# Second thread's state sums by transposes, and its first block prepared inside the leading thread's first layer

## The chip, the cores and the metric

The kernel runs on one core of a Trainium2 chip. The metric is the device time of one execution in microseconds (us). Before the change it was 4766.82 us, the median of three runs (4752.45, 4766.82 and 4772.51).

The engines go by short names. PE is TensorE with its matmuls, PEld its weight loads, DVE is VectorE, ACT is ScalarE, POOL is GpSimd, and SP is SyncE, whose queue issues almost all DMAs here.

## The reference, cut to what matters

A residual stream `x` of 8 sequences, 256 tokens and 256 features passes through twelve layers, each `x = x + layer(layernorm(x))`, with a context of 77 tokens beside it in some. All of it is in float32. The change concerns the first layer, a state-space layer that runs forwards and backwards:

```
def _s6(u, A_log, D, Wx, Wdt, bdt):
    A = -jnp.exp(A_log)
    dbc = jnp.einsum('bld,ed->ble', u, Wx)            # 64 of dt, 16 of B, 16 of C
    ...
    delta = jax.nn.softplus(jnp.einsum('blr,dr->bld', dt, Wdt) + bdt)
    dA = jnp.exp(delta[..., None] * A)
    dBu = delta[..., None] * Bm[:, :, None, :] * u[..., None]
    ...
        h = dA_t * h + dBu_t
        y = jnp.einsum('bdn,bn->bd', h, C_t)
    ...
    return ys + u * D
```

`u` is the input projection to 512 channels, convolved causally over four tokens and passed through Silu. Each of the 512 channels has 16 states. The two directions are added, multiplied by a gate (the Silu of the other half of the input projection) and by one half, and projected back to 256 features. The second layer is a cross attention over context and tokens (`perceiver16` in the kernel), the third a mixture of experts (`moe`).

## The kernel before

The eight sequences form four blocks of two (512 tokens each). Two Python generators, called threads here, issue the program: the leading one ("left") takes blocks 0 and 1 through all twelve layers, the second one ("right") blocks 2 and 3. `build` holds a planned time for each thread and always advances the one that is behind. Each `yield` of a layer moves its thread on by a step `dt`, derived from the layer's share in `SHARE`. The second thread starts with a lag of 1.01 x 470 planned units, which is about the planned end of the leading thread's first layer. The order in which instructions are traced is their priority. The tile framework then picks, for each engine, the ready instruction with the highest priority and so fixes each engine's queue; on the chip each queue runs in order. A tile pool hands its buffers out in that order too. Pools lie on the left or the right side of the on-chip memories, one side for each thread, and a new pool reuses the addresses of a closed one on its side, tile by tile.

**The leading thread's first layer** (class `Wide`) has the machine to itself and uses both sides: `net` (left) and `other` (right). `steps` prepares block 0 with `channels` (norm, transposes, projection, convolution by four products with diagonal `taps`, Silu), `rows` (the product with Wx into `dbc`, a copy of its B and C rows to DRAM as `rows0f`, and C turned into `cols`) and `delta` (softplus). After that each block has a forward and a backward "way" of 16 states by two halves. `way` issues half a state, and after it one more step of the `parts` that belong to a later stretch: gated products of the block before, gates of this one, and the channels, rows and delta of the next. In the last way (block 1, backwards) only the gates stand beside the states.

`state` makes, for each of four chunks of 128 channels: `st = exp(dl * A)` in PSUM on ACT (L825), `db = du * B` on POOL (L827), a scan on DVE (L829), and y. For three states out of four y is summed with tokens in rows: PE transposes the state (L854, `ht`), ACT scales it by C (L856, `ys`), and PE transposes it back into the accumulating bank (L859). For each fourth state DVE multiplies by C (L832, `hc`, two buffers), and PE adds the product up with the identity as weights (L833). The other products of this layer share the two `ht` banks through an alias.

**The second thread's first layer** (`ssm`, L541) starts when that one ends. It loads the layer's weights once more (L547), and for each block norms and turns x, projects and convolves (four DVE instructions per chunk, L565 and L569), applies Silu, makes `dbc` and writes the rows to DRAM. In its first block it also zeroes a table of slots for `moe` (`cleared`). Then it takes two chunks at a time (`c0`) and for each direction makes `dl` and `du` (L593 to L608) and 16 states x 2 chunks: a row load `rep` that is broadcast to all partitions (L614), `st` (L618), `db` on POOL (L622), the scan (L623), `hc` (L627, four buffers), and on PE

```
                            nc.tensor.matmul(
                                y[c],
                                lhsT=net.ident,
                                rhs=hc,
                                start=d == "f" and n == 0,
                                stop=d == "b" and n == 15,
                            )
```

at L628: the identity is the weight, hc streams through with 512 columns, and the bank `y[c]` holds channels in rows. The two `mm` banks serve both `st` and every other product of this layer. After both directions the gate is computed (L642), u is combined with y (L643, L646), and after the second pair the block is projected and added to x (`project`, L462).

Meanwhile the leading thread is in `perceiver16` (attention in head pairs; scores `sc`, maximum L966, exponentials L970, scaling L977, transposes L983, `av`), with one PSUM buffer of each kind.

Of the kernel before, what the change touches and what calls it, by code (L numbers as in the profile page):

```python
# [8 lines left out]
F32 = mybir.dt.float32  # L9
U8 = mybir.dt.uint8  # L10
I32 = mybir.dt.int32
AF = mybir.ActivationFunctionType
# [6 lines left out]
C = 77  # L19
# [271 lines left out]
def pairs_of(t):  # L291

    return t.rearrange("p (b t) -> p b t", b=2)


class Base:
# [25 lines left out]

    def load_rest(self):
        for blk in range(1, NB):
            self.load(blk)


class Net:
# [24 lines left out]
    def weights(self, i, split=1):  # L353
# [4 lines left out]
        t = self.work.tile([128, n + m], src.dtype, name=f"w{i}")  # L358
# [153 lines left out]
def context(base, room, net):  # L512
# [3 lines left out]
    rows = room.work.tile([C, B, D], F32, name="rows")  # L516
# [24 lines left out]
def ssm(net):  # L541


    nc = net.nc
    with net.scope(mm=2, y=1):
        work = net.work
        w = net.weights(0, 3)  # L547
# [7 lines left out]
        for blk in net.blks:  # L555
            xt = net.normed_turned(blk, bufs=1)
            u = work.tile([128, 4, 2, S], F32, name="u")
            for c in range(4):
                ps = net.bank()
                net.mms(ps, [(w["W_in"][:, k, c * 128 : c * 128 + 128], xt[:, k, :]) for k in range(2)])  # L560
                u0 = work.tile([128, 2, 3 + S], F32, name="u0", bufs=2)
                nc.gpsimd.memset(u0[:, :, 0:3], 0.0)
                nc.scalar.copy(u0[:, :, 3:], pairs_of(ps))
                acc = work.tile([128, 2, S], F32, name="acc", bufs=2)
                nc.vector.tensor_scalar(  # L565
                    acc, u0[:, :, 0:S], w["conv"][:, c, 0:1], w["b_conv"][:, c : c + 1], ALU.mult, ALU.add
                )
                for k in range(1, 4):
                    nc.vector.scalar_tensor_tensor(  # L569
                        acc, u0[:, :, k : k + S], w["conv"][:, c, k : k + 1], acc, ALU.mult, ALU.add  # L570
                    )
                nc.scalar.activation(u[:, c], acc, AF.Silu)
                yield
            dbc, rows = {}, {}
            for d in "fb":
                ps = net.bank()
                net.mms(pairs_of(ps[:96]), [(w[d + "Wx"][:, c, :], u[:, c]) for c in range(4)])
                dbc[d] = work.tile([96, 512], F32, name="dbc_" + d)
                nc.scalar.copy(dbc[d], ps[:96])

                rows[d] = net.base.dram.tile([32, 512], F32, name=f"rows{blk}{d}")
                nc.sync.dma_start(rows[d], dbc[d][64:96])
            if blk == net.blks[0]:
                yield from cleared(net, net)
            yield
            for c0 in range(0, 4, 2):
                y = [net.ps["y"].tile([128, 512], F32, name=f"y{c}") for c in range(2)]
                for d in "fb":
# [23 lines left out]
                    for n in range(16):  # L612
                        rep = work.tile([128, 2, 512], F32, name="rep", bufs=3)
                        nc.sync.dma_start(rep, by_state[n : n + 1].to_broadcast([128, 2, 512]))  # L614
                        for c in range(2):
# [12 lines left out]
                            nc.tensor.matmul(  # L628
                                y[c],
                                lhsT=net.ident,  # L630
                                rhs=hc,
                                start=d == "f" and n == 0,
                                stop=d == "b" and n == 15,
                            )
                            yield
                for m in range(2):
# [5 lines left out]
                    nc.scalar.activation(res, pairs_of(ps), AF.Silu)  # L642
                    nc.vector.scalar_tensor_tensor(  # L643
                        u[:, c], u[:, c], skip[:, c : c + 1], pairs_of(y[m]), ALU.mult, ALU.add
# [3 lines left out]
            for b in range(2):  # L648
                net.project(blk, b, u[:, :, b], w["W_out"])
                yield  # L650


class Wide:
# [8 lines left out]
    def steps(self):  # L662
        net, nc, other = self.net, self.nc, self.other
# [1682 lines left out]
```

## Time and profile before

| what | value |
|---|---|
| runs shown | 4752.45, 4766.82, 4772.51 us |
| profiled execution, its own time | 4753.15 us |
| its span, first to last instruction | 4751.4 us |
| PE, DVE, ACT, POOL busy | 86%, 56%, 42%, 33% of the span |
| mean granted PE clock | 0.909 |
| last wide scan, first scan of the second thread | 517.1 us, 589.1 us |
| second thread's eight runs of scans | 589.1 to 1306.0 us |
| loads of w0, w0 once more | 1.67 us, 533.5 us |

A line of the groups reads: source line, engine and operation, tiles out and in, shapes, count, then busy time, mean nanoseconds of one, and the idle time just before it with what ended it. A line of a stage table reads: from and to, length, busy time (and count) of each engine, granted clock, share of the DMA engines busy, GB/s. In the timeline a line has its start, its length, the instruction with its count, and in brackets the idle time before it and what ended that. A matmul in float32 appears as two instructions (passes), a transpose as one. Matmuls overlap in PE's pipeline, so a row of several is shorter than their sum.

### The profile page before, as it was taken

How to read it: one execution, taken by the hardware profiler on the slowest of the kernel's cores; microseconds unless marked ns; L12 is line 12 of the kernel's file. 1: busy time of each engine (PE TensorE's matmuls, PEld its weight loads, DVE VectorE, ACT ScalarE, POOL GpSimd, SP SyncE). 2: the span in 40 equal slices, each digit the busy share in tenths (PEclk: the TensorE clock that was granted, in tenths of full speed). 3: DMA queues.
4: the chain of work that ended last, by engine and by line, in shares of the span. 5: the costliest groups of instructions: out<-in, count | busy, mean ns of one | idle time of the engine just before them, and what ended most of it. 6: DMA issues, size and time to landing. Idle time of an engine off the chain costs nothing.

```text
span 4751.4 us, 54874 instructions
## 1 busy us (share of the span) xinstructions
PE 4087.7 (86%) x20192; PEld 2663.6 (56%) x20192; DVE 2665.2 (56%) x5064; ACT 2004.2 (42%) x4513; POOL 1576.2 (33%) x1373
## 2 busy tenths in 40 slices
PE   7777788887889899988989998788989999877988
PEld 3555433433347566655766665555556767645655
DVE  6768787767841444556254556665473562243355
ACT  6767465656533343432333342422343342233331
POOL 5758454344512411124442333432011001122123
PEclk8989899988989899998989998777889999988999
DMA  3111343233416100001610000100010000001000
GB/s 125 55 33 48 117 112 101 58 90 96 99 57 235 60 1 1 13 3 71 242 42 1 1 32 16 41 14 1 1 47 1 14 36 1 34 25 40 2 18 36
DMA packets 96319, 239.72 MB, mean 50 GB/s; under 512 B 8395, under 2 KB 36403, under 8 KB 85683
## 3 DMA queue, kind: packets, MB, share of 16 engines
q1 hardware_dynamic: 86355, 179.49, 12.2%
q0 software_dynamic: 9696, 56.72, 3.4%
q8 instruction: 160, 2.62, 0.2%
q14 instruction: 108, 0.88, 0.1%
HBM read 216.05 MB, written 20.14 MB: 50 GB/s over the span
## 4 chain that ended last, share of the span: by engine, by line
PE 46%; DVE 11%; POOL 5%; issue 4%; ACT 3%; DMA 1%; POOLq 0%; DVEq 0%; ACTq 0%
PE mm L395 22%; PE sc L395 5%; PE sc L403 5%; PE av L403 3%; PE pt L395 3%; PE o L395 3%; PE mm L983 1%; DVE xn L418 1%; PE mm L403 1%; PE mm L2175 1%; PE mm L428 1%; PE mm L1840 1%; DVE hn_sq L1897 1%; DVE pex L979 1%; POOL m_part L1596 1%
## 5 line engine op out<-in xcount | busy, mean ns | idle before, releaser
L622 POOL TENSOR_TENSOR db<-du,rep 128x512 f32<-128x512 f32 x256 | 320.2, 1271 | 182.6 <-DMA rep<-rows3f 44.2
L827 POOL TENSOR_TENSOR db<-du,rep 128x512 f32<-128x512 f32 x256 | 320.9, 1284 | 105.1 <-DVE h L829 81.9
L387 ACT COPY pv<-mm 111x384 f32<-111x384 f32 (+2 forms) x387 | 197.7, 512 | 331.6 <-PE mm L983 144.6
L395 PE MATMUL mm<-xt,w 128*128 128x512 f32 (+1 forms) x704 | 310.2, 569 | 30.7 <-issue 6.2
L623 DVE TENSOR_TENSOR_SCAN mm<-mm,db 128x512 f32<-128x512 f32 x256 | 310.7, 1222 | 36.7 <-ACT mm L618 20.9
L1333 POOL TENSOR_TENSOR qs<-q,w 128x256 f32<-128x256 f32 x256 | 155.4, 628 | 479.6 <-PE sc L395 479.0
L403 PE MATMUL sc<-k,q 64*128 64x333 f32 (+1 forms) x1152 | 249.5, 492 | 74.0 <-ACT pex L970 36.1
L628 PE MATMUL y<-hc,consts 128*128 128x512 f32 x512 | 279.1, 651 | 38.0 <-DVE hc L627 37.9
L403 PE MATMUL av<-pv,v 111*64 111x256 f32 (+5 forms) x2752 | 255.6, 384 | 16.3 <-ACT pv L387 9.2
L395 PE MATMUL sc<-k,qs 128*128 128x256 f32 x1024 | 265.8, 388 | 3.4 <-ACT ex L1347 1.6
L983 PEld LDWEIGHTS mm<-consts,pex 128*111 128x111 f32 x960 | 146.2, 195 | 195.5 <-issue 52.6
L983 PE MATMUL mm<-consts,pex 128*111 128x128 f32 x960 | 197.0, 316 | 61.8 <-ACT pex L977 18.5
L829 DVE TENSOR_TENSOR_SCAN h<-st,db 128x512 f32<-128x512 f32 x192 | 223.2, 1208 | 41.4 <-ACT st L825 34.4
L395 PE MATMUL mm<-h,sw 128*128 128x256 f32 x1024 | 243.3, 384 | 0.0
L970 ACT ACTIVATE pex<-sc,pnm 128x333 f32<-128x333 f32 x320 | 170.3, 537 | 139.3 <-DVE pnm L966 122.9
L403 PEld LDWEIGHTS sc<-k,q 64*128 64x128 f32 (+1 forms) x1152 | 111.8, 200 | 195.4 <-ACT pex L970 67.9
L395 PE MATMUL mm<-kv,w 128*128 128x256 f32 (+1 forms) x640 | 207.3, 445 | 13.3 <-ACT q L1024 10.8
L416 POOL TENSOR_TENSOR rs<-ve,neghalf 128x4 f32<-128x4 f32 (+1 forms) x57 | 59.2, 1039 | 476.3 <-DVE ve L414 395.1
L395 PEld LDWEIGHTS mm<-h,sw 128*128 128x128 f32 x1024 | 192.7, 193 | 32.9 <-issue 6.9
L395 PEld LDWEIGHTS mm<-xt,w 128*128 128x128 f32 x704 | 133.6, 206 | 136.4 <-issue 82.1
L395 PE MATMUL mm<-w,ao 128*128 128x256 f32 x768 | 197.5, 398 | 12.4 <-DVE x L462 10.8
L395 PEld LDWEIGHTS sc<-k,qs 128*128 128x128 f32 x1024 | 181.7, 192 | 45.2 <-issue 15.9
(482 smaller groups left out, 9073.4 us busy)
## 6 DMA issues: line engine op xcount, KB each, us to landing
rep<-rows2f SPq DMA_DIRECT2D x32, 512.0 KB
rep<-rows2b SPq DMA_DIRECT2D x32, 512.0 KB
rep<-rows3f SPq DMA_DIRECT2D x32, 512.0 KB
rep<-rows3b SPq DMA_DIRECT2D x32, 512.0 KB
w<-in_w SPq DMA_DIRECT2D x12, 1024.0 KB
w<-in_w SPq DMA_DIRECT2D x8, 1025.0 KB
w<-in_w SPq DMA_DIRECT2D x6, 1001.0 KB
w<-in_w SPq DMA_DIRECT2D x6, 838.0 KB
```

The costliest lines, as they stand in the source:

```text
L387: self.nc.scalar.copy(out, in_)
L395: self.nc.tensor.matmul(out, lhsT=lhs, rhs=rhs, start=n == 0, stop=n == len(pairs) - 1)
L403: self.nc.tensor.matmul(out, lhsT=lhs, rhs=rhs, start=start, stop=stop, tile_position=at)
L416: nc.gpsimd.tensor_tensor(rs[:rows], ve[:rows], self.neghalf[:rows, :n], ALU.pow)
L622: nc.gpsimd.tensor_tensor(db, du[:, c, :], rep[:, 0], ALU.mult)
L623: nc.vector.tensor_tensor_scan(st[:, order], st[:, order], db[:, order], 0.0, ALU.mult, ALU.add)
L628: nc.tensor.matmul(y[c], lhsT=net.ident, rhs=hc, start=d == "f" and n == 0, stop=d == "b" and n == 15,)
L827: nc.gpsimd.tensor_tensor(db, du[:, c, :], self.rep[:, 0], ALU.mult)
L829: nc.vector.tensor_tensor_scan(h[:, order], st[:, order], db[:, order], 0.0, ALU.mult, ALU.add)
L970: nc.scalar.activation(ex[:, e, :], sc[:, e, :NK], AF.Exp, bias=nm[:, e : e + 1], accum_out=sm[:, e : e + 1])
L983: nc.tensor.transpose(pt[:CH, j * 128 : j * 128 + 128], ex[:, e, j * CH : (j + 1) * CH], net.ident)
L1333: nc.gpsimd.tensor_tensor(qs[:, kc].rearrange("p n (h t) -> p n h t", h=H), q[:, kc, t0 : t0 + 16].rearrange("p (n t) -> p n t", n=2).unsq ...
```

## The change

It has two parts with what they need.

The second thread's `hc` is no longer streamed through the identity. Each of its four slices of 128 tokens is the weight of a transpose that adds into PSUM, so that the two y banks hold tokens in rows and both chunks of the pair in columns. At the end of the pair ACT copies both banks to SBUF (`yt`), and PE transposes them back before u is combined.

The second thread's block 2 goes through `channels` and `rows` in the leading thread's last way, as its `then` block, and not in `ssm`. Its `cols` and `delta` are left to the second thread, which needs no `cols`. The tiles that are handed over (weights, xt, u, dbc) lie in a new pool `shared` on the right side, which stays open until the second thread's `ssm` ends, so the weights are loaded once. `cleared` moves behind the first direction of the second thread's first pair. The context's `rows` tile takes the buffer of `res`.

```diff
+    def hand(self):
+        self.handed = ExitStack()
+        self.shared = self.handed.enter_context(
+            self.tc.tile_pool(name="shared", bufs=1, side="right", reuse_waits="tile")
+        )
...
 def context(base, room, net):
-    rows = room.work.tile([C, B, D], F32, name="rows")
+    rows = net.work.tile([128, 4, 512], F32, name="res").rearrange("p a (n c) -> p (a n) c", c=D)[:C]
...
 def ssm(net):
-        w = net.weights(0, 3)
+        shared, first = net.base.shared, net.base.first
+        w = first["w"]
...
         for blk in net.blks:
-            xt = net.normed_turned(blk, bufs=1)
...
+            if blk == net.blks[0]:
+                xt, u, dbc, rows = (first[k] for k in ("xt", "u", "dbc", "rows"))
+            else:
+                xt = shared.tile([128, 2, 512], F32, name="xt")
...
-            if blk == net.blks[0]:
-                yield from cleared(net, net)
             yield
             for c0 in range(0, 4, 2):
...
-                            nc.tensor.matmul(
-                                y[c],
-                                lhsT=net.ident,
-                                rhs=hc,
-                                start=d == "f" and n == 0,
-                                stop=d == "b" and n == 15,
-                            )
+                            for i in range(4):
+                                o = i % 2 * 256 + c * 128
+                                nc.tensor.matmul(
+                                    y[i // 2][:, o : o + 128],
+                                    lhsT=hc[:, i * 128 : i * 128 + 128],
+                                    rhs=net.ident,
+                                    is_transpose=True,
+                                    start=d == "f" and n == 0 and c == 0 and i % 2 == 0,
+                                    stop=d == "b" and n == 15 and c == 1 and i % 2 == 1,
+                                    skip_group_check=True,
+                                )
                             yield
+                    if blk == net.blks[0] and not c0 and d == "f":
+                        yield from cleared(net, net)
+                yt = work.tile([128, 4, 2, 128], F32, name="yt")
+                for i in range(2):
+                    nc.scalar.copy(yt[:, 2 * i : 2 * i + 2], y[i].rearrange("p (i c m) -> p i c m", i=2, c=2))
                 for m in range(2):
...
+                    ps = net.bank()
+                    for i in range(4):
+                        nc.tensor.transpose(ps[:, i * 128 : i * 128 + 128], yt[:, i, m, :], net.ident)
                     nc.vector.scalar_tensor_tensor(
-                        u[:, c], u[:, c], skip[:, c : c + 1], pairs_of(y[m]), ALU.mult, ALU.add
+                        u[:, c], u[:, c], skip[:, c : c + 1], pairs_of(ps), ALU.mult, ALU.add
                     )
...
+    net.base.handed.close()
...
 class Wide, steps:
+        self.base.hand()
-            self.w = w = net.weights(0, 3)
+            self.w = w = net.weights(0, 3, self.base.shared)
...
                         parts.append(self.gates(now))
+                        parts += [self.channels(then), self.rows(then, "f"), self.rows(then, "b")]
                         if blk != net.blks[-1]:
-                            parts += [self.channels(then), self.rows(then, "f"), self.rows(then, "b")]
                             parts.append(self.delta(then, "f"))
...
+            self.base.first = dict(now, w=w)
...
+    def of(self, o):
+        return self.net.work if o["blk"] in self.net.blks else self.base.shared
...
 Wide.rows:
         yield
+        if o["blk"] not in net.blks:
+            return
```

Where `Wide` allocates xt, u and dbc it now asks `of(o)` for the pool and takes one buffer there in place of two.

## The prediction

> **What bounds the kernel now.** I read the page first, then a table of stages, then what VectorE (DVE) waits for in the stage that the change touches.
>
> ```profile
> PE 4087.7 (86%) x20192; PEld 2663.6 (56%) x20192; DVE 2665.2 (56%) x5064; ACT 2004.2 (42%) x4513; POOL 1576.2 (33%) x1373
> ...
> L623 DVE TENSOR_TENSOR_SCAN mm<-mm,db 128x512 f32<-128x512 f32 x256 | 310.7, 1222 | 36.7 <-ACT mm L618 20.9
> ...
> L628 PE MATMUL y<-hc,consts 128*128 128x512 f32 x512 | 279.1, 651 | 38.0 <-DVE hc L627 37.9
> ```
>
> By the page PE is the engine to relieve: it is busy 86% of the span, and L628, which the change replaces, is one of its largest groups. The table of stages (us; busy time of PE, PEld, DVE, ACT, POOL; granted clock; DMA share) says something else.
>
> ```profile
> 158.00:292.00 134.00, 108.88 (x497) 65.95 (x496) 88.86 (x88) 98.89 (x143) 79.61 (x67) 0.94 0.14 41
> ...
> 421.00:517.00 96.00, 75.66 (x430) 52.90 (x428) 82.23 (x79) 75.49 (x118) 74.94 (x63) 0.95 0.17 50
> ...
> 531.00:589.00 58.00, 37.58 (x86) 15.64 (x86) 34.81 (x107) 20.22 (x31) 9.21 (x12) 0.75 0.59 204
> ...
> 671.00:735.00 64.00, 53.74 (x178) 23.82 (x176) 61.14 (x76) 39.15 (x83) 39.01 (x32) 0.96 0.46 123
> ...
> 905.00:977.00 72.00, 64.40 (x239) 35.17 (x238) 26.51 (x47) 47.87 (x86) 3.87 (x5) 0.91 0.08 24
> ```
>
> 158:292 and 421:517 are the backward directions of the wide thread's two blocks. 531:589 is the second thread's start. 671:735 is one of its eight runs of 32 scans (two chunks, one direction): DVE is busy 61.1 of 64 us. 905:977 lies between its two blocks. The waits of DVE from 590 to 1310 us (total, times, longest):
>
> ```profile
> DVE mm L623 <- ACT mm L618: 20.9, 39, 1.5
> ...
> DVE hc L627 <- PE y L628: 0.5, 2, 0.3
> ```
>
> In the second thread's ssm DVE sets the pace inside the runs, and it waited for the y sums 0.5 us in 720. Between runs a chain over ACT, DVE and POOL does: the gaps from last to first scan are 15.1 to 16.6 us between directions, 21.2 and 31.7 between chunk pairs, 72.4 between blocks. Only after 1415 us is PE the limit (2970 busy of 3336 us).
>
> **1. The y sums by transposes (L628).** Starts in the timeline give the real cost of a row:
>
> ```profile
> 204.29 0.60 PE L859 MATMUL y<-consts,ys 128*128 128x128 f32 x4
> ...
> 1045.30 1.88 PE L628 MATMUL y<-hc,consts 128*128 128x512 f32 x4
> ```
>
> Four passes of 512 columns take 1.88 us, one alone 0.59, so one takes (1.88-0.59)/3 = 0.43, and an hc, which needs two, 0.86. Four 128-column transposes take 0.60, one alone 0.27, so (0.60-0.27)/3 = 0.11 each and 0.44 for the four that replace an hc. PE gets back 0.42 x 256 = 107 us. Weight loads go from two of 189 ns to four of 141 ns (row L859), beside other PE work: PEld is busy 24 of 64 us in a run. On the second thread's chain this is worth 0: 32 x (1.222 + 0.686) = 61.1 us of DVE work per run stay. Who can use the 107 us is the leading thread, in perceiver16 beside the runs. Bound of its gain: a y pass is on PE 0.86/1.91 = 45% of the time, so its PE work waits 0.45 x 0.43 = 0.19 us on average, afterwards 0.23 x 0.22 = 0.05; with nine dependent PE steps in a head pair and 28 pairs from 590 to 1310 that is up to -35. But its pace does not depend on y: two maxima (L966) in nearly each 20 us of a run, and ten in the 105 us from 1310 to 1415, when there is no y any more. I take -8 for the leading thread.
>
> The clock may answer. PE busy in a run falls from 53.7 to about 53.7 - 32 x 0.42 = 40 of 64 us (63%). Row 531:589, with 65%, has a granted clock of 0.75; row 421:517, where turning transposes (L854, L859) are most of PE's work, has 0.95. I take a small loss, +3 for the leading thread; the full one is a rival. [...]
>
> **2. The end of a chunk pair.** Added, four times: two PSUM copies of 0.59 us on ACT (as L387 copies of 128x512) and eight transposes in two lots of 0.60, ahead of L643; the two mm banks now serve four products in place of two before the next delta gets one. The next pair's first y waits for the copies in place of L643. I take +2 each, +8 on the second thread's chain; bounds 0 (the gates' table load and Silu, L642, are late anyway) and +5 each, +20.
>
> **3. The prologue of block 2 goes.** The last wide scan ends at 517.1, the second thread's first starts at 589.1: 72 us. What remains is the constants and one delta chain, which needs only the wide thread's last st banks and far tiles; a direction gap (15.1 to 16.6 us, the same chain) is the nearest row, so 16 plus 2 for neg_a: 18. The gain is 54, less 3 because DVE then also holds the leading thread's norms (34.8 of 58 us busy): -51. W0 (three loads of 838 KB) is not loaded again: its 2.5 MB stood behind the leading thread's w1 on SP's queue and nobody waited for it at 551.8, when the first product waited for DVE, so 0. The zeroing of the slot table (2.9 MB) moves from 535 us into the gap after the first run, ahead of that direction's first rep loads on the same queue: at 373 GB/s it takes 8 us, the gap is 15.9; +2, bounds 0 and +8.
>
> **4. The same work in the wide thread's last direction.** This is what I look at hardest. The parts added there are channels and two rows; the first block's backward direction has these and a delta besides. From scans to scans it took 133.9 us (158.1 to 292.0), the last direction without them 96.4 (420.6 to 517.1). Ceiling: +37.5. Two DVE stalls are most of it:
>
> ```profile
> 218.81 0.69 DVE L832 TENSOR_TENSOR hc<-st,rep 128x512 f32<-128x512 f32 x1 [10.66 <-PE y L833]
> ...
> 260.15 0.69 DVE L832 TENSOR_TENSOR hc<-st,rep 128x512 f32<-128x512 f32 x1 [12.51 <-PE y L833]
> ```
>
> An hc tile (two buffers) stays occupied because its y product is queued on PE behind the products of channels and rows, which wait for ht banks and ACT. Queued behind it stand the scans, and POOL's db behind those. SP gets two writes of 64 KB between its rep loads, POOL one power of 1.0 us and four memsets of 0.1; they are in the rows' difference. Both stalls come from parts that the change adds: 10.7 + 12.5 = 23; I take +24, bounds 0 (DVE is idle 14% of that direction) and +37.5. Everything behind the direction moves with it: the last gated product and the leading thread's w1 load, which today is issued at 530.7. The context's rows, now in the buffer of res, cost 0: ctx_nrm leaves at 120.2, and res is first written at 183.0.
>
> **The sum.** Second thread: -51 + 24 + 8 + 2 = -17. Leading thread: +24 for its later start; from 551.8 to 577 its products no longer share PE with 32 of the other's passes (32 x 0.43 = 14) and DVE with 17 us of norm and convolution, partly the same time, -17; -8 and +3 from part 1: +2. Behind them PE is 89% busy and serves both, so being ahead in one thread is worth about half: (-17 + 2)/2 = -8. The profiled run took 4753.15 (span 4751.4 and 1.75 around it) and would take 4745. It is near the lowest of the three shown (4752.45); against their median, 4766.82, I forecast **4759**. No change is what a measurement cannot tell from it, 0.5% or 24 us.
>
> **Rivals.** *Freed time is used*: the wide thread takes the preparation almost for nothing (+5), since its last direction has six spare k-steps after the rows, and the leading thread gets all of -35. Second thread -51 + 5 + 8 + 2 = -36; leading thread +5 - 17 - 35 = -47; mean -42: 4725, and 4705 if the PE-bound stretch 905:977 (64.4 of 72) shrinks too. For it: 107 us of the busiest engine. Against: DVE's 0.5 us and the constant pace of L966.
>
> *The clock falls* (the slower side): one mechanism, in the second thread's runs. If PE at 63% gets 0.75, as in 531:589, the leading thread's PE work there (53.74 - 31.8 of y = 22 us a run, some 7 a head pair) grows by 7 x (1/0.75 - 1/0.94) = 1.9 us, over 28 pairs +53 in place of +3, and 905:977 by about 14. Second thread -3, leading +52, mean +25: 4792; at 0.70, 4802. It decides from 0.75 down.
>
> *It does not do what it says*: the prepared delta still waits for tiles of the wide thread or its parts run after the last scan, so the 72 us stay a 72 us prologue in another order: 4767 to 4780.
>
> **Chances.** Forecast 0.49, time used 0.29, clock 0.16, not as said 0.06. Faster by over 0.5%: 0.29 + 0.01 of the forecast = 0.30. Slower: 0.16 + 0.02 of the last = 0.18. The rest, 0.52, within. The range leaves out the outer third of both rivals: 4705 to 4802.
>
> **What would show it.** Right: scans of the last wide direction spread over some 120 us with one or two DVE stalls on y of 10 us; first scan of the second thread about 18 us after the last wide one; its runs still 64 to 69 us at DVE 95%, PE in them near 63%; chunk-pair gaps 23 or more. Wrong: runs shorter than 62 us (then y did bind), a last direction under 105 us, a granted clock in the runs under 0.8, or a distance of L966 pairs clearly under 20 us, which would mean that the leading thread did wait for PE.

## The result, and the profile after

The changed kernel takes 4794.74 us, the median of eleven runs (4781.47 to 4803.45); the kernel before took 4767.62 beside it, also in eleven (4747.35 to 4790.5). The ratio is 1.0057, with a 95% interval of 1.0041 to 1.0073: slower by 27 us, just past the 0.5% that the forecast called no change. The profiled execution took 4782.94 us (span 4781.2), 12 less than the median, so late times read from it are some us too early.

The page's sums, and the second thread's scans (now L635) and y sums (L643):

```profile
PE 4065.9 (85%) x20768; PEld 2749.3 (58%) x20768; DVE 2664.8 (56%) x5047; ACT 1997.7 (42%) x4516; POOL 1578.8 (33%) x1373
...
L635 DVE TENSOR_TENSOR_SCAN mm<-mm,db 128x512 f32<-128x512 f32 x256 | 307.7, 1221 | 38.6 <-ACT mm L630 27.7
...
L643 PE MATMUL y<-consts,hc 128*128 128x128 f32 x1024 | 185.1, 325 | 50.5 <-DVE hc L639 50.1
```

The y sums cost PE 185 us where they cost 279, that is 94 less. But PE as a whole is only 22 us less busy: its other work keeps it busy some 70 us longer, and the granted clock is lower. The table of stages (columns as before) shows where:

```profile
160.00:297.00 137.00, 110.20 (x496) 66.69 (x495) 90.65 (x92) 98.26 (x142) 79.99 (x68) 0.93 0.13 40
425.00:552.00 127.00, 103.14 (x504) 63.60 (x502) 83.25 (x80) 91.57 (x137) 75.35 (x64) 0.97 0.13 39
552.00:589.00 37.00, 14.87 (x56) 9.51 (x56) 26.37 (x76) 8.42 (x12) 10.41 (x11) 0.72 0.60 209
679.00:747.00 68.00, 53.91 (x256) 36.00 (x252) 62.09 (x76) 42.26 (x90) 40.23 (x33) 0.76 0.46 113
925.00:996.00 71.00, 64.23 (x252) 35.61 (x250) 26.01 (x47) 49.18 (x89) 4.38 (x6) 0.90 0.10 25
```

The last wide direction takes 126.7 us (425.4 to 552.0) where it took 96.4. From its end to the second thread's first scan pass 37 us, so that this scan starts at 589.4, where it started at 589.1 before. A run of scans (679:747) has a granted clock of 0.76 where it had 0.96. The eight runs sum to 536.9 us, before to 527.5. What DVE waits for from 590 to 1316 us has no row for y:

```profile
DVE dl L614 <- ACT du L612: 30.0, 7, 7.8
DVE mm L635 <- ACT mm L630: 27.7, 60, 1.5
```

In the last wide direction the timeline of DVE has the two long stalls that the prediction took over from block 0:

```profile
487.38 0.69 DVE L869 TENSOR_TENSOR hc<-st,rep 128x512 f32<-128x512 f32 x1 [10.62 <-PE y L870]
...
528.07 0.69 DVE L869 TENSOR_TENSOR hc<-st,rep 128x512 f32<-128x512 f32 x1 [11.86 <-PE y L870]
```

And these are the steps between the last wide scan and the first of the second thread:

```profile
560.42 0.26 ACT L560 ACTIVATE nega_f<-w 128x64 f32<-128x64 f32 x1 [7.70 <-DVE u L929]
...
565.70 1.98 SPq L369 DMA_DIRECT2D w<-in_w  x4
...
567.86 0.74 DVE L610 TENSOR_SCALAR dl<-mm,w 128x512 f32<-128x512 f32 x1
568.44 1.72 SPq L626 DMA_DIRECT2D rep<-rows2f  x3
...
582.49 3.79 POOL L634 TENSOR_TENSOR db<-du,rep 128x512 f32<-128x512 f32 x3
582.55 4.20 DVE L425 TENSOR_SCALAR xn<-x,mv,rs 128x256 f32<-128x256 f32 x4 [1.12 <-POOL rs L423]
...
589.41 2.33 DVE L635 TENSOR_TENSOR_SCAN mm<-mm,db 128x512 f32<-128x512 f32 x2
```

`dl` (L610) waits on DVE behind the last gated sums. The first row loads `rep` (L626) stand on SP's queue behind w1 (L369, 4 MB), which waits for the wide thread's last tiles (33.0 us, for the products into `ht`, L402). The first `db` comes 14 us after its load was issued, and then the leading thread's norms are ahead of the scan on DVE.

Up to the end of `perceiver16`, which the loads of each thread's next layer mark, little is lost. The leading thread's next load (w2) is issued at 1396 us in place of 1386, the second thread's (w1) at 1318 in place of 1331. So the gap of 27 us opens later.

### The profile page after: what moved, and what is told of

It reads as the page before. It is cut to its first block, busy times and chain, and to the rows that moved or that the text cites. A ratio compares the mean times of both kernels' runs of the same rounds, so it can differ in the third digit from the quotient of the medians.

```text
span 4781.2 us, 55998 instructions
## 1 busy us (share of the span) xinstructions
PE 4065.9 (85%) x20768; PEld 2749.3 (58%) x20768; DVE 2664.8 (56%) x5047; ACT 1997.7 (42%) x4516; POOL 1578.8 (33%) x1373
## 4 chain that ended last, share of the span: by engine, by line
PE 47%; DVE 12%; POOL 4%; issue 4%; ACT 3%; DMA 1%; another core or an unknown queue 1%; POOLq 0%; SPq 0%; ACTq 0%; DVEq 0%
PE mm L402 23%; PE sc L410 5%; PE sc L402 5%; PE av L410 4%; PE pt L402 3%; PE o L402 2%; PE mm L1020 2%; DVE xn L425 1%; PE mm L435 1%; PE mm L2212 1%; DVE hn_sq L1934 1%; PE mm L410 1%; PE mm L1564 1%; DVE st L418 1%
## 5 line engine op out<-in xcount | busy, mean ns | idle before, releaser
L635 DVE TENSOR_TENSOR_SCAN mm<-mm,db 128x512 f32<-128x512 f32 x256 | 307.7, 1221 | 38.6 <-ACT mm L630 27.7
L402 PE MATMUL mm<-xt,w 128*128 128x512 f32 (+1 forms) x688 | 289.1, 550 | 36.7 <-DVE rope_s L1321 11.8
L410 PE MATMUL av<-pv,v 111*64 111x256 f32 (+5 forms) x2752 | 278.9, 406 | 19.3 <-ACT pv L394 13.7
L1020 PE MATMUL mm<-consts,pex 128*111 128x128 f32 x960 | 215.6, 340 | 93.3 <-ACT pex L1014 32.9
L402 PE MATMUL sc<-k,qs 128*128 128x256 f32 x1024 | 263.9, 386 | 2.9 <-POOL k L1323 1.8
L402 PE MATMUL mm<-h,sw 128*128 128x256 f32 x1024 | 245.8, 385 | 0.0
L643 PE MATMUL y<-consts,hc 128*128 128x128 f32 x1024 | 185.1, 325 | 50.5 <-DVE hc L639 50.1
L402 PE MATMUL mm<-kv,w 128*128 128x256 f32 (+1 forms) x640 | 216.5, 462 | 12.6 <-ACT q L1061 5.1
L410 PEld LDWEIGHTS av<-pv,v 128*32 128x32 f32 (+3 forms) x2752 | 133.9, 141 | 140.3 <-issue 57.7
L402 PE MATMUL mm<-w,ao 128*128 128x256 f32 x768 | 204.3, 407 | 7.7 <-DVE x L469 6.5
L402 PEld LDWEIGHTS mm<-h,sw 128*128 128x128 f32 x1024 | 192.1, 193 | 32.2 <-issue 7.5
L402 PEld LDWEIGHTS sc<-k,qs 128*128 128x128 f32 x1024 | 180.0, 190 | 46.0 <-issue 18.3
L643 PEld LDWEIGHTS y<-consts,hc 128*128 128x128 f32 x1024 | 147.0, 168 | 100.5 <-DVE hc L639 78.5
```

The costliest lines, as they stand in the source:

```text
L402: self.nc.tensor.matmul(out, lhsT=lhs, rhs=rhs, start=n == 0, stop=n == len(pairs) - 1)
L410: self.nc.tensor.matmul(out, lhsT=lhs, rhs=rhs, start=start, stop=stop, tile_position=at)
L635: nc.vector.tensor_tensor_scan(st[:, order], st[:, order], db[:, order], 0.0, ALU.mult, ALU.add)
L643: nc.tensor.matmul(y[i // 2][:, o : o + 128], lhsT=hc[:, i * 128 : i * 128 + 128], rhs=net.ident, is_transpose=True, start=d == "f" and n ...
L1020: nc.tensor.transpose(pt[:CH, j * 128 : j * 128 + 128], ex[:, e, j * CH : (j + 1) * CH], net.ident)
```

## The experiments

My theory was that the preparation is the loss (it lengthens the last wide direction and delays the leading thread, and SP's and DVE's queues take back what the second thread gains). Its rivals were that the clock is the loss, and that the order of the later layers is. A ratio is the time beside the kernel before on the same chip. The clock is the mean of the timed runs' granted clocks; the other columns (us) are from one profile each: the leading thread's first maximum in `perceiver16`, the second thread's first scan, and the issue of the second thread's w1 and the leading thread's w2.

| kernel | ratio (95%) | clock | maximum | scan | w1, w2 |
|---|---|---|---|---|---|
| before | 1 | .909 | 593 | 589 | 1331, 1386 |
| after | 1.0057 (1.0041 to 1.0073) | .885 | 622 | 589 | 1318, 1396 |
| e_trans | 0.9987 (0.9967 to 1.0006) | .893 | 592 | 588 | 1317, 1380 |
| e_prep | 1.0084 (1.0058 to 1.0109) | .902 | 633 | 568 | 1325, 1425 |
| e_dummy | 1.0024 (1.0008 to 1.0040) | .908 | 619 | 587 | 1419, 1354 |
| e_dummy16 | 1.0062 (1.0039 to 1.0086) | .890 | 620 | 587 | 1325, 1399 |
| e_td128 | 0.9991 (0.9971 to 1.0011) | .911 | 586 | 583 | 1329, 1346 |
| e_hc4 | 1.0088 (1.0064 to 1.0112) | .903 | 634 | 570 | 1325, 1422 |
| e_split | 1.0061 (1.0037 to 1.0084) | .888 | 620 | 587 | 1316, 1394 |
| e_rep | 1.0070 (1.0050 to 1.0089) | .904 | 629 | 564 | 1314, 1410 |
| e_lead | 1.0035 (1.0018 to 1.0052) | .908 | 612 | 608 | 1347, 1402 |
| e_sec | 1.0016 (0.9997 to 1.0034) | .909 | 607 | 604 | 1343, 1398 |
| e_lag8 | 1.0039 (1.0021 to 1.0058) | .894 | 620 | 587 | 1316, 1394 |
| e_lag20 | 1.0013 (0.9998 to 1.0029) | .891 | 622 | 589 | 1318, 1396 |
| e_lag32 | 1.0104 (1.0080 to 1.0129) | .882 | 621 | 589 | 1321, 1399 |
| e_before_m8 | 1.0027 (1.0011 to 1.0044) | .901 | 597 | 583 | 1332, 1387 |
| e_before_p20 | 1.0066 (1.0045 to 1.0087) | .905 | 574 | 593 | 1325, 1380 |
| e_prep_lag20 | 1.0078 (1.0053 to 1.0102) | .906 | 633 | 569 | 1325, 1422 |
| e_dummy_lag20 | 0.9985 (0.9972 to 0.9998) | .913 | 622 | 589 | 1416, 1355 |
| e_dummy128_lag20 | 0.9992 (0.9979 to 1.0005) | .909 | 620 | 588 | 1329, 1376 |

### One part at a time

**e_trans** is the kernel before with the change's y sums (`is_transpose`, `yt` and its way back), **e_prep** the kernel after with those of before:

```diff
-                            for i in range(4):
-                                o = i % 2 * 256 + c * 128
...
-                                    is_transpose=True,
...
+                            nc.tensor.matmul(
+                                y[c],
+                                lhsT=net.ident,
+                                rhs=hc,
...
```

> The kernel before with one part of the change alone: the second thread's y sums by transposes with tokens in rows, copied and turned back at the end of a chunk pair. Block 2 keeps its prologue, the table is zeroed where it was. Theory 'preparation' (the loss comes from the work moved into the wide thread's last direction and from what that makes late): 4755 to 4775, that is at most +8 for the pair ends and a little back from PE time. Theory 'clock' (transposes lower the granted clock in the second thread's runs): the clock from 600 to 1300 us falls from .92 to about .8, the runs sum to some 537 in place of 527 us, and the time is 4785 to 4800, nearly the whole loss of the change.

> The kernel after with y streamed through the identity as before: only the preparation of block 2 in the wide thread's last direction is left of the change. Theory 'preparation': last direction 127 us, leading thread's first maximum at some 620 in place of 593, second thread's first scan at 589 all the same, time 4785 to 4800. Theory 'clock': the same places, but the clock in the runs is back at .92 and the time within 8 of the kernel before (4760 to 4775).

The transposes alone change nothing that can be measured (-0.13%), although the clock falls as it does in the kernel after. Nor does the low clock lengthen the runs of scans there: the eight sum to 525.9 us, where before they took 527.5. The preparation alone is slower by 0.84%, by the intervals at least about as much as the whole change. So the loss comes with the preparation. This is not yet my theory shown: these kernels also have the shift in the plan that the preparation brings (see the order of the later layers).

It also shows what the shorter prologue is worth. In e_prep SP has the first row loads ahead of w1, and the first scan comes 16 us after the last wide one, 21 us earlier than before the change. SP's queue in e_prep:

```profile
539.84 13.23 SPq L626 DMA_DIRECT2D rep<-rows2f  x3
553.17 0.42 SPq L934 DMA_DIRECT2D slots_right<-zero  x1
566.10 2.06 SPq L369 DMA_DIRECT2D w<-in_w  x4
```

But the first run then takes 86.1 us and ends at 654.6, where before the change it also ended at 654.6. Engines in that run (e_prep), and in the prologue and the first run of before:

```profile
568.00:655.00 87.00, 59.93 (x146) 25.05 (x146) 79.84 (x137) 31.22 (x57) 44.02 (x37) 0.80 0.47 139
```

```profile
531.00:589.00 58.00, 37.58 (x86) 15.64 (x86) 34.81 (x107) 20.22 (x31) 9.21 (x12) 0.75 0.59 204
589.00:655.00 66.00, 54.75 (x180) 24.65 (x181) 61.88 (x77) 40.22 (x85) 40.01 (x33) 0.91 0.45 117
```

In e_prep's run DVE has 137 instructions and is busy 80 of 87 us; before it had 77 and was busy 62 of 66. The leading thread's norms, which used to lie beside the prologue, now lie in the run.

### The clock

**e_dummy** is the kernel after with one product more for each hc, which adds zeros; **e_dummy16** has 16 columns in it, and **e_td128** is e_trans with 128.

```diff
+        zeros = work.tile([128, 128], F32, name="zeros")
+        nc.gpsimd.memset(zeros, 0.0)
...
+                            nc.tensor.matmul(
+                                y[c][:, :256],
+                                lhsT=zeros,
+                                rhs=hc[:, :256],
+                                start=False,
+                                stop=False,
+                                skip_group_check=True,
+                            )
```

> The kernel after, and with each hc one product more that adds nothing: 256 columns of hc with a weight of zeros into the y bank, so that PE is about as busy in the runs as before the change (some 0.43 us more for each hc, 110 us in all). Theory 'clock': the granted clock in the runs comes back from .79 to .9 or more, the runs sum to under 530 us, and the time falls 10 to 25 below the kernel after (4770 to 4785) although PE has more to do. Theory 'preparation': the clock may come back, but the time stays at that of the kernel after (4790 to 4800) or rises.

> The kernel after, with the product that adds nothing on 16 columns in place of 256: the instruction and its place are there, hardly any PE activity. If the 20 us gained by 256 columns came from the granted clock, this kernel keeps the clock of .8 in the runs and takes the time of the kernel after (4790 to 4800). If they came from another order of the two threads' instructions, it takes 4770 to 4780 at the low clock.

> The kernel before with y by transposes alone, and with the product that adds nothing on 128 columns for each hc (55 us of PE in all, half of what the transposes gave back). Theory 'clock': with the transposes alone the clock in the runs was .8 and the time -0.1% of the kernel before; with some more PE activity the clock is .87 or more and the time 10 to 20 below the kernel before (ratio 0.996 to 0.998). If the clock does not matter, the added work shows as +0 to +10 (ratio 0.999 to 1.001).

More work for PE makes the kernel after faster, from 1.0057 to 1.0024 (the two intervals just touch), and 16 columns do not (1.0062). The granted clock in the table goes with it. From 600 to 700 and 1000 to 1100 us, after and then e_dummy:

```profile
600.00:700.00 100.00, 73.35 (x313) 46.89 (x314) 80.55 (x109) 58.84 (x120) 51.22 (x41) 0.75 0.36 97
1000.00:1100.00 100.00, 79.49 (x330) 49.28 (x330) 83.07 (x103) 57.60 (x111) 54.45 (x44) 0.77 0.41 109
```

```profile
600.00:700.00 100.00, 81.81 (x418) 52.56 (x416) 82.47 (x107) 60.00 (x122) 52.74 (x43) 0.93 0.41 99
1000.00:1100.00 100.00, 80.67 (x399) 53.21 (x400) 75.42 (x99) 65.28 (x131) 52.86 (x42) 0.85 0.33 86
```

If the clock is the reason, it costs the changed kernel some 0.33%, 16 us, and that net of the added work. But this is not shown: e_dummy's queues have another order (all 64 maxima before the last scan, 56 in the kernel after), its runs did not shorten as expected (543.0 us in all), the leading thread gains 42 us by the end of `perceiver16` (w2 at 1354) and the second one loses 101 (w1 at 1419). e_dummy16, whose counts are nearly those of the kernel after, is the control for the extra instruction, not for that order. Without the preparation the clock is worth nothing that shows: e_td128 has it back (.911) at half the added work, and 0.9991 is not below e_trans; that expectation failed.

### What the preparation costs, and where

**e_hc4** is e_prep with four buffers in place of two for the wide `hc`, and three in place of four for `db` to make room (the edit shown; a tile of zeros also moves into an `hc` buffer). **e_split** is the kernel after with `channels(then)` in block 1's forward direction. **e_rep** is e_prep with three early loads on another queue.

```diff
-                db = far.tile([128, 512], F32, name="db", bufs=4)
+                db = far.tile([128, 512], F32, name="db", bufs=3)
...
-                    hc = far.tile([128, 512], F32, name="hc", bufs=2)
+                    hc = far.tile([128, 512], F32, name="hc", bufs=4)
```

> The preparation alone (y streamed through the identity), with four buffers in place of two for the wide thread's hc, to make room three in place of four for its db, and the zero tile of the leading thread's table in one of the hc buffers. Theory 'preparation': DVE's two stalls of 10.6 and 11.9 us on y in the last direction shrink to under 4 each, the direction goes from 127 to 105 to 112 us, the leading thread starts 15 to 20 earlier, and the time is 10 to 20 below the preparation alone. If these stalls cover work that takes as long in any case (ACT and the ht banks), the direction stays over 120 and the time is that of the preparation alone.

The second of the two cases came, not my theory's. The direction takes 123.6 us in place of 126.6, and the time is that of e_prep. What DVE waits for in that direction, in e_prep and then in e_hc4:

```profile
DVE hc L858 <- PE y L859: 24.6, 3, 11.9
DVE h L855 <- ACT st L851: 15.3, 16, 3.2
```

```profile
DVE h L855 <- PE ht L880: 24.7, 5, 8.9
DVE h L855 <- ACT st L851: 11.8, 9, 3.2
```

The 25 us have gone from hc to h, whose buffers wait for their transposes on the same PE queue. So it is not the number of hc buffers: PE's queue is held up behind the products of the preparation, and the next tile in line shows it.

```diff
                         parts.append(self.delta(now, "b"))
+                        if blk == net.blks[-1]:
+                            parts.append(self.channels(then))
...
-                        parts += [self.channels(then), self.rows(then, "f"), self.rows(then, "b")]
+                        if blk != net.blks[-1]:
+                            parts.append(self.channels(then))
+                        parts += [self.rows(then, "f"), self.rows(then, "b")]
```

> The kernel after, with the preparation spread: norm, projection and convolution of block 2 in block 1's forward direction, its rows in the last one. If the products of the preparation cost their time wherever they stand, the two directions together take what they took (248 us, 218 before the change) and the time is that of the kernel after. If it is the crowding of one direction, they take 225 to 235 together, the leading thread starts 12 to 20 earlier, and the time falls as much (4770 to 4785).

The two directions take 245 us with the gap between them (304.9 to 549.9), 250 in the kernel after, 219 before the change. Spread out, the preparation costs nearly the same, and the time does not change.

```diff
-                        nc.sync.dma_start(rep, by_state[n : n + 1].to_broadcast([128, 2, 512]))
+                        early = blk == net.blks[0] and not c0 and d == "f" and n < 3
+                        queue = nc.gpsimd if early else nc.sync
+                        queue.dma_start(rep, by_state[n : n + 1].to_broadcast([128, 2, 512]))
```

> The preparation alone (y streamed through the identity), with the row loads of the second thread's first three states issued from POOL's queue in place of SP's, where the 4 MB of w1 and the 2.9 MB of zeros stand. With the preparation alone the first scan came 16 us after the last wide one, but the first run took 86 us and ended at 655 as before the change. If SP's queue lengthens that run, it takes 66 to 72 us, ends at 635 to 642, and the time is 5 to 15 below the preparation alone (4790 to 4800). If it is DVE, which has the leading thread's norms to do in that stretch, the run stays over 80 us and the time at 4800 or more.

The first run takes 86.6 us as in e_prep, so SP's queue is not what lengthens it. The time, 1.0070, is not told apart from e_prep's by the intervals.

### What a late start is worth

**e_lead** is the kernel before with a chain on block 0 of x at the end of the wide layer; **e_sec** has the same chain on `x[2]` at the second thread's start.

```diff
+            nc.vector.scalar_tensor_tensor(self.base.x[0], self.base.x[1], 0.0, self.base.x[0], ALU.mult, ALU.add)
+            for _ in range(10):
+                nc.gpsimd.tensor_scalar(self.base.x[0], self.base.x[0], 1.0, None, ALU.mult)
```

> The kernel before, with block 0 of x held up by a chain of eleven instructions that change nothing (one on DVE that waits for block 1's last sum, ten on POOL of some 3.4 us): only the leading thread is late, by about 34 us, as in the changed kernel; its w1 load and the second thread are not held up. My forecast's rule for delays (one thread's delay counts half): +17, some 4780. Theory 'the leading thread sets the end': +30 or more, 4795 to 4805. Theory 'slack': within 8 of the kernel before.

> The kernel before, with the same chain on block 2 of x: only the second thread is late, by about 20 to 34 us at its first scan. By the rule of halves +10 to +17, 4772 to 4784. Theory 'the leading thread sets the end', by which an earlier second thread is worth nothing: within 8 of the kernel before (4755 to 4772).

e_lead gives +17 us, the number of the rule of halves, but not its reason. The chain, expected to take 34 us, takes some 30 (its POOL instructions 2.8 us each), and makes the leading thread 19 late and, against the expectation, the second thread 19 late too. In e_sec both are 14.5 late. Here the threads were coupled through their shared queues: the one that was made late at 590 us held up the other by as much (19 and 14.5 us), and what both are late by is found again at the end (+17) or partly so (+8, interval -1 to +16).

### The order of the later layers

The change takes four steps from the second thread's first layer (the four yields of its projection; that of `cleared` only moved). In the plan that fixes priorities this thread ends its first layer 453.1 units after its own start in place of 459.6 and is 6.5 units early in every layer that follows. **e_lag8, e_lag20, e_lag32** are the kernel after with a later planned start, **e_before_m8** and **e_before_p20** the kernel before with an earlier and a later one.

```diff
-            [lag, 1, thread(base, (2, 3), "right", run, (total - FIRST + SHARE[0]) / (total - lag))],
+            [lag + 20, 1, thread(base, (2, 3), "right", run, (total - FIRST + SHARE[0]) / (total - lag))],
...
-                first[0] = t + (lag if first[1] else 0.0)
+                first[0] = t + (lag + 20 if first[1] else 0.0)
```

> The kernel after, with the second thread's planned start put 8 units later. With four steps of its first layer gone, the second thread stands some 6.5 units earlier in the plan than before, in this and all later layers (it ends its first layer at 453.1 units in place of 459.6), and so its instructions go ahead of the leading thread's more often. If this order is what loses time, the leading thread's first maximum comes 5 to 10 us earlier than 622 and the time falls 8 to 20 (4770 to 4785 where the kernel after takes 4790). If the loss is only the leading thread's late start behind the longer direction, it stays within 6 of the kernel after.

> The kernel after, with the second thread's planned start 20 units later: the leading thread's norms and attention go first on every engine, and the second thread's first scan comes 10 to 30 us later. If the end follows the leading thread's start (as in the kernels so far: first maximum 593, 612, 622, 633 with ends of 0, +18, +27, +40), the time falls with the first maximum, to 4770 to 4785. If the two threads count alike, the second one's loss eats that: 4790 to 4805.

> The kernel after, with the second thread's planned start 32 units later. Shifts of 0, 8 and 20 gave ratios of 1.0057, 1.0039 and 1.0013 with the same first 1396 us. If the order of the later layers fits better the later the second thread stands, the ratio goes on to 0.997 to 1.000; if 20 was near the best place, it is 1.001 to 1.005.

> The kernel before, with the second thread's planned start 8 units earlier, about the shift that the change brings by the second thread's four missing steps (6.5 units). Theory 'order' (the shift puts the later layers' instructions in a worse order, whatever the first layer does): +8 to +25 us (ratio 1.002 to 1.005). Theory 'start' (only the later start of the leading thread counts, and 20 units helped the kernel after by undoing that): within 6 of the kernel before (ratio 0.999 to 1.001).

> The kernel before, with the second thread's planned start 20 units later, the same shift that took the kernel after from +0.57% to +0.13%. If the shift helps because the changed kernel's plan no longer fits its start, the kernel before, whose plan fits, gains nothing from it: ratio 0.999 to 1.005. If later is better in any case, it gains as much: ratio 0.995 to 0.997.

e_lag20 has the kernel after's first 1396 us to within 1 us (first maximum, first scan, w1 and w2 in the table) and ends at 1.0013. My expectation had the place wrong: the first layer did not change, the later ones did. e_before_m8 has the first 2390 us of the kernel before, nearly, and ends at 1.0027. Issue of three later loads: the second thread's fourth layer, then two of the leading thread's later layers.

| kernel | us | us | us |
|---|---|---|---|
| before | 2390 | 2769 | 3121 |
| e_before_m8 | 2389 | 2780 | 3154 |
| after | 2407 | 2800 | 3151 |
| e_lag20 | 2402 | 2776 | 3105 |

A shift alone, with no work moved, makes the kernel before late by 33 us at the third load, where the kernel after is 30 late. That is one thread's place and not yet the loss: the second thread's load of its sixth layer comes at 3051 us in e_before_m8 and 3078 in the kernel after, where before it came at 3066. The clock is lower there too. The stretch 3200 to 3500 us of before, e_before_m8, after and e_lag20:

```profile
3200.00:3500.00 300.00, 271.77 (x1260) 157.10 (x1258) 164.42 (x326) 94.87 (x221) 46.79 (x38) 0.81 0.03 13
```

```profile
3200.00:3500.00 300.00, 278.65 (x1165) 155.73 (x1164) 151.71 (x301) 86.92 (x179) 43.48 (x35) 0.72 0.03 13
```

```profile
3200.00:3500.00 300.00, 275.55 (x1212) 158.49 (x1212) 156.15 (x312) 91.41 (x191) 43.56 (x35) 0.76 0.03 13
```

```profile
3200.00:3500.00 300.00, 273.62 (x1302) 160.99 (x1300) 158.80 (x305) 104.10 (x218) 35.83 (x30) 0.80 0.01 2
```

PE is busier at the lower clock and gets through fewer instructions (1165 and 1212, against 1260 and 1302); the four kernels stand at different places of their work there, so how much of the loss is the clock's is not shown. The order has no simple direction: 8 units (1.0039) are not told apart from none, 32 give 1.0104, and 20 harm the kernel before (1.0066), both outside all that I expected.

**e_prep_lag20** is e_prep with the shift of 20.

> The preparation alone (y streamed through the identity) with the second thread's planned start 20 units later, the shift that took the kernel after from 1.0057 to 1.0013. If the shift mends the order of the later layers in the same way, the ratio goes from 1.0084 to about 1.004; what is then left above 1 (some 19 us) is the price of the 39 us by which the leading thread is late at 1425 us. If order and start depend on each other, any other value, 1.006 to 1.010 among them.

It stays at 1.0078: what this shift is worth depends on the kernel it meets, and the price of the preparation alone cannot be split in this way.

### Both remedies

**e_dummy_lag20** is e_dummy with the shift of 20, **e_dummy128_lag20** the same with 128 columns.

> The kernel after, with both edits that lowered it: the product that adds nothing on 256 columns, and the second thread's planned start 20 units later. If the granted clock in the runs and the order of the later layers are separate losses, the gains add (1.0057 - 0.0033 - 0.0044 = 0.998, some 10 us below the kernel before). If the 256 columns helped only by another order, they do not add: 1.001 to 1.003.

> The kernel after with the planned start 20 units later, and the product that adds nothing on 128 columns in place of 256. With 256 columns the ratio was 0.9985 at a clock of .914. If 128 columns already hold the clock, as they did in the kernel before with transposes alone (.911), half of the added PE work is saved: 0.995 to 0.998. If they do not, or the order of the first layer changes with them, 0.999 to 1.003.

The two gains add up as expected: 0.9985, the only version with an interval below 1, by 0.15%, and below the kernel after by some 0.7%. With 128 columns it is 0.9992, which the intervals do not tell apart from 256.

## Why the prediction was wrong

The time lies in the range; the sign does not fit the forecast (within 0.5%), by a hair: +0.57%.

*What bounds.* Right: DVE sets the pace of the runs before and after; with 94 us less of y sums on PE the eight runs together did not get shorter (527.5 before, 536.9 us after). The 0.5 us of waits for y are those inside the runs; at the ends of the pairs `u` (L643) waited 6.4 us more for it.

*Part 1.* The direction was right, the sizes were off. An hc costs PE 0.72 us (185.1 over 256) in place of 1.09 by the profile's busy times, 0.37 less where I took 0.42. But I let PE's share of a run fall to 63%, and it stayed at 53.9 of 68 us, 79%, at a clock that fell from between .90 and .95 to between .75 and .86 in stretches of 100 us. My +3 for the clock may be too small: the product that holds the clock gained some 16 us (e_dummy, where the order changed too), but e_trans lost nothing at the low clock. My reason for a small loss, the .95 of the row 421:517, was poor: one stage of transposes does not speak for another. In the kernel after the stage 425:552, where three of four states are summed by transposes, kept .97, and the run 679:747, where all are, had .76 (the last section has the count).

*The rival "the clock falls"* gave 4792 and came within 3 us of the median, and its sign, a clock under 0.8 in the runs, was seen (0.76). But that it came so near is luck: e_trans has the same low clock (.74 to .84 in the runs) and is not slower than before, and in the kernel after the leading thread's first 64 maxima took 759 us where before they took 778, not 50 us more.

*Part 2.* +2 for each pair end: the gaps between pairs went from 21.2 to 24.3 and from 31.7 to 28.2. About nothing.

*Part 3.* The 18 us from the last wide scan to the first of the second thread were 37 in the kernel after. I left out what stands ahead of this chain on two queues: w1 on SP's ahead of the first row loads, and on DVE the leading thread's sums and norms, ahead of `dl` (at 567.9 us, in e_prep at 561.0) and of the scan. e_prep, with 16 us, shows that the chain is as short as I took it, and also that the -51 was not there to be had: the prologue's 58 us were the leading thread's time for norms on DVE, and an earlier run only moves into them. The zeroing of the table cost 3 us in the gap (15.9 to 19.2), as forecast (+2).

*Part 4.* +24 was +30.3, inside the bound of 37.5, with stalls of 10.6 and 11.9 us where I took 10.7 and 12.5. The mechanism was PE's queue, as said; the two hc buffers were only where it showed. The directions before it ended 4.8 us later too (425.4 us for 420.6), which the sum had at nothing; no run separates why.

*The sum is the step that failed.* At the end of `perceiver16` I was close: the second thread 13 us early (forecast 17), the leading one 10 late (forecast 2), a mean of -2 where I had -8. "Behind them PE is 89% busy and serves both, so being ahead in one thread is worth about half" then put all that follows at half of each thread's lead, and the end came at +27. The other kernels fail this rule too, by the table's w1 and w2 against before: e_td128 has a mean of -21 and ends at -4 us, e_before_p20 -6 and +31, e_prep +17 and +40, e_dummy +28 and +11; only e_lead, a plain delay, fits (+16 and +17). The step took the later layers as they were and put a change in their order at nothing. But the change shifts the second thread in the plan by 6.5 units, and with it the order of later queues. The runs showed what such shifts do: 8 units alone cost the kernel before 0.27% (13 us), and 20 units take the kernel after from 1.0057 to 1.0013 with the same first 1396 us (21 us). With either the shift of 20 or the product of 256 columns the changed kernel would have been inside my "no change"; with both it is at 0.9985. That the 6.5 units themselves make up the 27 us is not shown, since shifts both ways cost the kernel before, 13 us (8 units earlier) and 31 us (20 later).

*What stays open:* which instructions change places in the later layers to cost the time, how e_dummy's gain divides between clock and order, and why the preparation alone, whose second thread is 6 us early and leading thread 39 late at the end of `perceiver16`, ends 40 us late, with the shift of 20 units or without it.

## What to carry to other kernels

A prologue on one thread is not idle time when another thread's work lies beside it: before counting it as gained, list what the other thread does on each engine and queue in that stretch. Where priorities come from a plan in steps, an edit that adds or removes steps moves everything behind it, so run the unchanged kernel with the plan shifted by that much: that is the scatter against which a change of 0.5% is to be read. And work taken from PE where another engine sets the pace can come back as a lower clock for what remains (.81 in e_trans from 600 to 1300 us, .92 before), which need not cost time: e_trans was no slower.

## What the runs showed of the hardware

The clock record of before and after has two values, full clock and half clock (1.0 and 0.5), and each of its stretches lasts a whole number of steps of 3.41 us. I added up, for each such step, the columns of the matmuls that start in it, transposes included, at 0.84 ns a column, which is 0.43 us for a pass of 512 as measured before the change. From 590 us to the end of the runs some 10% of the steps of the kernel before hold less than 0.4 of their length, and 17% are at half clock; after the change it is 26% and 39%. In the kernel after 96% of these steps with less than 0.4 are followed by one at half clock, and 19% of the others. In the last wide direction of the kernel after (425 to 552 us) 2 of 38 steps hold less than 0.4, and 2 are at half clock. Steps might also hold little because they are at half clock themselves. So these are the steps at full clock alone, over the whole execution, by what they hold of their length, and how many of them are followed by one at half clock:

| kernel | under 0.4 | 0.4 to 0.5 | 0.5 or more |
|---|---|---|---|
| before | 73, of these 80% | 32, 50% | 1031, 2% |
| after | 71, of these 90% | 39, 41% | 973, 2% |

Transposes count in this: over the whole execution of the kernel after 117 steps hold 0.5 or more with their transposes and less than 0.4 without, and 3% of them are followed by half clock. So in these two traces the clock goes with the columns in each short step. It does not go with the share of PE's busy time: from 600 to 1300 us PE is busy 543 of 700 us in the kernel after, 544 in e_trans and 544 in e_td128, and the clock is .80, .81 and .92. With 128 added columns for each hc, e_td128 has the .92 of the kernel before.

Within one kernel the time goes with the mean clock: in the 26 runs of the kernel before beside e_lag20 the granted clock went from .905 to .915 and the time from 4768 to 4730 us, some 40 us for 0.01. Between kernels it does not: e_trans, at .893 where the kernel before has .909, is no slower.
